# Gated graph network with attention on one core: sigmoid written through tanh, its affine part moved into VectorE's products

## The chip, the cores and the metric

The kernel runs on one core of one Trainium2 chip. The metric is device time in microseconds for one execution. A core has engines with queues of their own: TensorE (PE; its weight loads are PEld), VectorE (DVE), ScalarE (ACT), GpSimd (POOL) and SyncE (SP, which issues the DMAs). Each works through its queue in order and waits at semaphores for the others.

## The reference, cut to what matters

There are 128 graphs of 128 nodes with 256 features, in fp32, and an adjacency of zeros and ones for each graph. Layer 0 is a gated graph network of three rounds with shared gate weights, layer 1 an attention.

```python
h = jnp.maximum(_layernorm(x, axis=-1), 0.0)
for i in range(3):
    m = jnp.einsum('bnd,de->bne', h, weight[i])
    aggr = jnp.einsum('bst,bsd->btd', A, m)
    gi = aggr @ w_ih.T + b_ih;  gh = h @ w_hh.T + b_hh      # 3 * 256 columns each
    r = jax.nn.sigmoid(i_r + h_r)
    z = jax.nn.sigmoid(i_z + h_z)
    n = jnp.tanh(i_n + r * h_n)
    h = (1.0 - z) * n + z * h
x = x + h
h = jnp.maximum(_layernorm(x, axis=-1), 0.0)
Wh = h @ W;  s = Wh.sum(axis=-1)
e = jax.nn.leaky_relu(s[:, :, None] + s[:, None, :], negative_slope=0.2)
alpha = jax.nn.softmax(jnp.where(adj == 0, -jnp.inf, e), axis=-1)
return x + alpha @ Wh
```

## The kernel before

The 128 graphs are worked in 32 groups of four (`G = 4`). A group goes through three rounds, `layer` 0 to 2, so there are 96 phases (group, round). The list `turns` interleaves them: in the middle one phase each of group g, round 0; of g-1, round 1; and of g-2, round 2. A phase's gate products are planned at `SLOT` = 18150 ns of PE.

In rounds 0 and 1 the state is held transposed, in `hT` (features on the partitions, two halves j of 128, and 512 columns of four graphs times 128 nodes); in round 2 (`gru_rows`) the products come out with nodes on the partitions. `edge_sums` gives `aT`, the neighbours' sums, with matmuls in bf16 on three parts of each fp32 value. `node_sums` makes four sums and differences of blocks of `hT` and `aT` on POOL and DVE (`hs`, `gs`). From these `products` builds the gates by a scheme of seven block products in place of eight, in fp32 on PE. Its PSUM banks are X, Y and Q, each with one bank for r and z (`x_rz`, `y_rz`, `q_rz`) and one for the two parts of n (`x_n`, `y_n`, `q_n`: half 0 is h_n, half 1 is i_n). ACT copies X into Y (L702), and twice copies what Y holds to SBUF, as `t2` and `t3` (L692, `put`), while PE goes on adding to the same Y bank; DVE adds Q to these (L695). The four blocks that result lie in `T3`, `X`, `Y` and `T2`.

Then the gates, for each of the four blocks (j, n) in `gru`: ACT makes r with a sigmoid into `rz` (L740), DVE makes u = (h_n + bias) r (L743) and adds i_n (L747), and ACT makes z with another sigmoid (L750). For each half j ACT takes tanh of `u` (L756), and DVE makes d = h - n, d = d z and h = n + d (L759, L762, L764). `gru_rows` does the same with one sigmoid for r and z (L778), L782 and L786 for u, L795 for tanh and L797, L802 and L804 at the end; its biases are in PSUM already, since ACT seeds the banks with them (L687). `attention` follows the third round; its softmax takes the exps on ACT (L910).

The order of all engines is not that of the code: each `op(engine, ns, ...)` only notes an operation with a cost, and `Plan.run` orders them by a simulation, with PE's gate products at due times (`due`), the rest by how soon it is needed, and banks handed out in turn. The `exps` operation has a place of its own, right behind the copy of x_rz to y_rz of group g+2, round 1 (`turn=`), and its cost holds 2570 ns beside the exps for all groups but the last. `two=True` marks operations of DVE and POOL that the plan keeps from running at once.

Of the kernel before, what the change touches and what calls it, by code (L numbers as in the profile page):

```python
# [12 lines left out]
AF = mybir.ActivationFunctionType  # L13
OP = mybir.AluOpType
AX = mybir.AxisListType

P = 128
# [193 lines left out]
def kernel(  # L211
# [60 lines left out]
        "s_hh": (1, "all", const, [P, 7, 3, P]), "s_x0": (1, "all", const, [P, 7, 3, P]),  # L272
        "s_x1": (1, "all", const, [P, 7, 3, P]), "s_x2": (1, "all", const, [P, 7, 3, P]),
        "bias_i": (1, "all", const, [P, 3 * KD]), "bias_h": (1, "all", const, [P, 3 * KD]),
        "bias_s": (1, "all", const, [P, 3 * KD]),
        "seed_x": (1, "all", const, [P, 4, P]), "seed_q": (1, "all", const, [P, 4, P]),
        "w1": (1, "all", const, [P, KD, D]), "w1_out": (1, "all", const, [P, KD]),
        "w1_sum": (1, "all", const, [P, D]),
# [12 lines left out]
    def ap(b):  # L291
        return phys[(b.tag,) + b.slot]
# [13 lines left out]
    for kind in ("y_rz", "y_n"):  # L306
        y = phys[kind, 0, 0].rearrange("p q n -> p (q n)")
        for c in range(GN // P):
# [1 line left out]
                             skip_group_check=True)  # L310


    W = {t: buf(t) for t in ("s_hh", "s_x0", "s_x1", "s_x2", "bias_i", "bias_h", "bias_s", "seed_x",
                             "seed_q", "w1", "w1_out", "w1_sum")}
    spare = ["misc", "x_rz", "misc", "x_n", "misc", "q_rz", "misc", "q_n"]

# [56 lines left out]
    def weights():  # L373
# [18 lines left out]
        load_msg(1)  # L392
        for t, src in (("bias_i", b_ih), ("bias_h", b_hh)):
            load(W[t], ap, src.rearrange("(c p) -> p c", p=P), 500)
        op("DVE", 170, lambda: nc.vector.tensor_add(ap(W["bias_s"]), ap(W["bias_i"]),
                                                    ap(W["bias_h"])),
           [W["bias_i"], W["bias_h"]], [W["bias_s"]])

        w_hhT, w_ihT = [buf("u"), buf("u")], [buf("x1"), buf("x1")]
        turned(w_ih_nat, w_ihT, ("DVE", "ACT"))  # L400
# [271 lines left out]
    def products(layer, hT, hs, aT, gs, rows=False):  # L672

        five, seven, three, four = (7, 5, 4, 3) if rows else (5, 7, 3, 4)
        state, edges = (W["s_hh"], hT, hs), (W[f"s_x{layer}"], aT, gs)  # L680
        kinds = (("rz", ((R, (state, edges)), (Z, (state, edges)))),
                 ("n", ((NN, (state,)), (NN, (edges,)))))
        X, Y, Q, T2, T3 = ({} for _ in range(5))

        def seed(b, kind, t):
            q = 0 if kind == "rz" else 2
            op("ACT", 590, lambda: nc.scalar.copy(  # L687
                ap(b), ap(t)[:, q:q + 2].rearrange("p (o q) m -> p o (q m)", o=1)
                .to_broadcast([P, 2, 2 * P])), [t], [b])

        def put(t, y):
            op("ACT", 590, lambda: nc.scalar.copy(ap(t), ap(y)), [y], [t])  # L692

        def add(t, q):
            op("DVE", 690, lambda: nc.vector.tensor_tensor(ap(t), ap(t), ap(q), OP.add), [q], [t])  # L695

        for kind, parts in kinds:
            X[kind], Y[kind] = buf("x_" + kind), buf("y_" + kind)
            if rows:
                seed(X[kind], kind, W["seed_x"])  # L700
            product(X[kind], 1, parts, not rows, rows=rows)
            op("ACT", 590, lambda x=X[kind], y=Y[kind]: nc.scalar.copy(ap(y), ap(x)),  # L702
               [X[kind]], [Y[kind]], mark=(plan.group, layer, kind))
        for kind, parts in kinds:
            Q[kind] = buf("q_" + kind)
            if rows:
                seed(Q[kind], kind, W["seed_q"])
            product(Q[kind], five, parts, not rows, rows=rows)
        for kind, parts in kinds:
            product(Y[kind], 6, parts, False, rows=rows)  # L710
            T2[kind] = buf("t2_" + kind)
            put(T2[kind], Y[kind])
        for kind, parts in kinds:
            product(Y[kind], seven, parts, False, rows=rows)
            T3[kind] = buf("t3_" + kind)
            put(T3[kind], Y[kind])
# [10 lines left out]
        return (1, 1, T3), (0, 0, X), y + (Y,), t2 + (T2,)  # L727

    def gru(layer, hT, hs, aT, gs):

        blocks = products(layer, hT, hs, aT, gs)
        rz, u = buf("rz"), buf("u")

        def view(b, q=None):
            t = ap(b) if q is None else ap(b)[:, q]
            return t.rearrange("p (j n m) -> p j n m", j=KD, n=2)
        for j, n, src in blocks:
            cr, cz, cn, i = j, KD + j, 2 * KD + j, 2 * j + n
            s_rz, nn = src["rz"], src["n"]
            op("ACT", 511, lambda j=j, n=n, s_rz=s_rz, c=cr: nc.scalar.activation(  # L740
                view(rz, 0)[:, j, n, :], ap(s_rz)[:, 0, :], AF.Sigmoid, bias=ap(W["bias_s"])[:, c:c + 1]),
               [s_rz, W["bias_s"]], [(rz, i, i + 1)])
            op("DVE", 480, lambda j=j, n=n, nn=nn, c=cn: nc.vector.scalar_tensor_tensor(  # L743
                view(u)[:, j, n, :], ap(nn)[:, 0, :], ap(W["bias_h"])[:, c:c + 1], view(rz, 0)[:, j, n, :],
                op0=OP.add, op1=OP.mult), [nn, (rz, i, i + 1), W["bias_h"]], [(u, i, i + 1)],
               two=nn.tag[0] == "t")
            op("DVE", 422, lambda j=j, n=n, nn=nn: nc.vector.tensor_tensor(  # L747
                view(u)[:, j, n, :], view(u)[:, j, n, :], ap(nn)[:, 1, :], OP.add),
               [nn], [(u, i, i + 1)], two=nn.tag[0] == "t")
            op("ACT", 500, lambda j=j, n=n, s_rz=s_rz, c=cz: nc.scalar.activation(  # L750
                view(rz, 1)[:, j, n, :], ap(s_rz)[:, 1, :], AF.Sigmoid, bias=ap(W["bias_s"])[:, c:c + 1]),
               [s_rz, W["bias_s"]], [(rz, 4 + i, 5 + i)])
        for j in (1, 0):
            d, lo, hi = buf("d"), 2 * j, 2 * j + 2
            cols = slice(j * GN, (j + 1) * GN)
            op("ACT", 723, lambda j=j, cols=cols: nc.scalar.activation(  # L756
                ap(u)[:, cols], ap(u)[:, cols], AF.Tanh,
                bias=ap(W["bias_i"])[:, 2 * KD + j:2 * KD + j + 1]), [W["bias_i"]], [(u, lo, hi)])
# [3 lines left out]
            op("DVE", 690, lambda d=d, cols=cols: nc.vector.tensor_tensor(  # L762
                ap(d), ap(d), ap(rz)[:, 1, cols], OP.mult), [(rz, 4 + lo, 4 + hi)], [d], two=True)
            op("DVE", 690, lambda j=j, d=d, cols=cols: nc.vector.tensor_tensor(  # L764
                ap(hT)[:, j, :], ap(u)[:, cols], ap(d), OP.add), [(u, lo, hi), d], [(hT, lo, hi)], two=True)

    def gru_rows(layer, hT, hs, aT, gs, rows, x1):

        blocks = products(layer, hT, hs, aT, gs, rows=True)
        rz, u = buf("rz"), buf("u")  # L770

        def view(b):
# [1 line left out]
        for j, n, src in blocks:  # L774
# [2 lines left out]
            s_rz, nn = src["rz"], src["n"]  # L777
            op("ACT", 700, lambda outs=outs, graphs=graphs, s_rz=s_rz: nc.scalar.activation(  # L778
                ap(rz).rearrange("p q (g d) -> p g q d", g=G)[:, graphs, :, outs],
                ap(s_rz).rearrange("p g (q m) -> p g q m", q=2), AF.Sigmoid),  # L780
               [s_rz], [(rz, i, i + 1), (rz, 4 + i, 5 + i)])
            op("DVE", 422, lambda outs=outs, graphs=graphs, nn=nn: nc.vector.tensor_tensor(  # L782
                view(u)[:, graphs, outs], ap(nn)[:, :, 0:P],
                ap(rz)[:, 0].rearrange("p (g d) -> p g d", g=G)[:, graphs, outs], OP.mult),
               [nn, (rz, i, i + 1)], [(u, i, i + 1)], two=nn.tag[0] == "t")
            op("DVE", 422, lambda outs=outs, graphs=graphs, nn=nn: nc.vector.tensor_tensor(  # L786
                view(u)[:, graphs, outs], view(u)[:, graphs, outs], ap(nn)[:, :, P:2 * P], OP.add),
               [nn], [(u, i, i + 1)], two=nn.tag[0] == "t")
        for n in (1, 0):
            d, lo, hi = buf("d"), 2 * n, 2 * n + 2  # L790
# [2 lines left out]
            def part(b, lo=lo, hi=hi):  # L793
# [8 lines left out]
            op("DVE", 690, lambda d=d, cols=cols: nc.vector.tensor_tensor(  # L802
                ap(d), ap(d), ap(rz)[:, 1, cols], OP.mult), [(rz, 4 + lo, 4 + hi)], [d], two=True)
            op("DVE", 690, lambda d=d, part=part: nc.vector.tensor_tensor(  # L804
                part(x1), part(x1), ap(d), OP.add), [d], [(x1, lo, hi)], two=True)


    turns = [(0, 0), (1, 0), (2, 0), (0, 1), (1, 1), (3, 0), (0, 2), (2, 1), (1, 2)]
# [51 lines left out]
    def attention(g, a, x1, h1, lo, hi):  # L860
# [47 lines left out]
        def exps():  # L908
            for b in range(lo, hi):
                nc.scalar.activation(ap(e)[:, b, :], ap(e)[:, b, :], AF.Exp, bias=ap(low)[:, b:b + 1])  # L910
        op("ACT", 2570 * (g < NG - 1) + 320 * n, exps, [low], [e], turn=(g + 2, 1, "rz"))
        op("DVE", cost, lambda: nc.vector.tensor_reduce(small(den), es(), AX.X, OP.add), [e], [den])
        op("DVE", 170, lambda: nc.vector.reciprocal(small(rden), small(den)), [den], [rden])
        eT, uT = buf("eT"), buf("uT")
# [80 lines left out]
```

## Time and profile before

| | us |
|---|---|
| median of 3 runs | 2139.39 |
| lowest and highest | 2138.39, 2139.82 |
| the profiled execution | 2138.75 |
| its span, first to last instruction | 2136.9 |
| granted clock of TensorE, mean | 0.995 |

| engine | busy us | share |
|---|---|---|
| PE | 2108.1 | 99% |
| PEld | 1879.9 | 88% |
| DVE | 1750.7 | 82% |
| ACT | 1587.1 | 74% |
| POOL | 951.0 | 45% |

The shares are means over the whole span. Matmuls are pipelined, and their ends are modelled in the profile, so that the spacing of their starts says more than the busy time. Among the groups of ACT is ACT_TABLE_LOAD, an instruction that no line of the kernel writes: it is put before an activation whose function is not in the table set that the engine holds at that moment. A group's time is told with its count and the mean duration of one instruction; a "wait" is idle time of an engine before an instruction, put down to what ended it.

### The profile page before, as it was taken

Reading aid. Unit: us, or ns where it says so; the run is one execution under the profiler, and the core shown is the slowest. Engines: PE = TensorE matmul, PEld = TensorE weight load, DVE = VectorE, ACT = ScalarE, POOL = GpSimd, SP = SyncE. Lnnn points to the kernel's source line nnn. Section 1 sums busy time; section 2 is a strip of 40 time slices with the busy share of each in tenths; the row PEclk is TensorE's granted clock in tenths of the full one; section 3 lists DMA queues with packets and bytes.
Section 4 is the critical chain, followed back from the end, with each engine's and each line's share of the span. In section 5 each row is a group of like instructions: output and inputs, shape, how many; then the busy total and the mean of one; then the engine's idle time right before and its main releaser. Section 6 shows DMA issues by size and latency. Waiting matters only on the chain.

```text
span 2136.9 us, 33989 instructions
## 1 busy us (share of the span) xinstructions
PE 2108.1 (99%) x12550; PEld 1879.9 (88%) x12550; DVE 1750.7 (82%) x3297; ACT 1587.1 (74%) x2705; POOL 951.0 (45%) x889
## 2 busy tenths in 40 slices
PE   8999999999999999999999999999999999999997
PEld 7889888898888988889988889888888988988886
DVE  5677878788888889888898788888889888778777
ACT  5567877777877877777877777777777888676774
POOL 5545453445544445544344544355444454335421
PEclk9999999999999999999999999999999999999998
DMA  4222223232242312332222231313223323222221
GB/s 143 45 50 50 45 50 89 45 77 48 45 89 60 75 37 49 79 70 65 55 62 56 68 75 40 94 32 69 65 51 84 46 38 82 50 46 37 59 68 35
DMA packets 333430, 129.35 MB, mean 61 GB/s; under 512 B 264656, under 2 KB 333008, under 8 KB 333264
## 3 DMA queue, kind: packets, MB, share of 16 engines
q1 hardware_dynamic: 333264, 127.18, 27.1%
q8 instruction: 99, 1.62, 0.3%
q14 instruction: 67, 0.55, 0.1%
HBM read 45.36 MB, written 16.78 MB: 29 GB/s over the span
## 4 chain that ended last, share of the span: by engine, by line
PE 94%; DVE 3%; ACT 1%; DMA 1%; issue 1%; SPq 0%; DVEq 0%; ACTq 0%
PE y_rz L655 15%; PE q_rz L655 10%; PE x_rz L655 10%; PE y_rz L662 8%; PE y_n L655 7%; PE misc L597 6%; PE q_rz L662 5%; PE x_n L655 5%; PE x_rz L662 5%; PE q_n L655 5%; PE misc L935 5%; PE y_n L662 4%; PE misc L611 3%; PE x_n L662 3%; PE q_n L662 3%; PE misc L892 1%
## 5 line engine op out<-in xcount | busy, mean ns | idle before, releaser
L692 ACT COPY t_rz<-y_rz 128x512 f32<-128x512 f32 x192 | 112.3, 585 | 200.5 <-PE y_rz L662 104.9
L557 POOL TENSOR_TENSOR r<-rows 128x512 f32<-128x512 f32 x128 | 148.2, 1177 | 221.1 <-ACT rows L540 121.6
L625 POOL TENSOR_TENSOR hs<-hT 128x512 f32<-128x512 f32 x96 | 131.3, 1368 | 183.7 <-PE y_n L662 126.7
L655 PE MATMUL y_rz<-hs,s_hh 128*128 128x256 f32 x768 | 198.0, 380 | 2.6 <-ACT t_rz L692 2.6
L655 PE MATMUL y_rz<-gs,s_x 128*128 128x256 f32 x768 | 197.1, 379 | 0.0
L695 DVE TENSOR_TENSOR t_rz<-t_rz,q_rz 128x512 f32<-128x512 f32 x192 | 131.3, 684 | 69.4 <-PE q_rz L662 26.0
L582 POOL TENSOR_TENSOR pl<-d,pl 128x512 bf16<-128x512 f32 x64 | 77.9, 1219 | 217.8 <-ACT pl L580 217.7
L560 POOL TENSOR_TENSOR p<-r 128x512 bf16<-128x512 f32 x128 | 168.1, 1332 | 0.0
L655 PEld LDWEIGHTS y_rz<-gs,s_x 128*128 128x128 f32 x768 | 146.0, 190 | 19.8
L655 PEld LDWEIGHTS y_rz<-hs,s_hh 128*128 128x128 f32 x768 | 141.5, 190 | 21.8 <-ACT t_rz L692 4.0
L799 POOL TENSOR_TENSOR x<-x,u 128x512 f32<-128x512 f32 x64 | 88.1, 1379 | 143.0 <-ACT u L795 140.1
L695 DVE TENSOR_TENSOR t_n<-t_n,q_n 128x512 f32<-128x512 f32 x192 | 131.3, 684 | 22.5 <-ACT t_n L692 8.5
L629 POOL TENSOR_TENSOR hs<-hT,hs 128x256 f32<-128x256 f32 x96 | 74.1, 773 | 149.4 <-PE q_n L662 130.7
L577 POOL TENSOR_TENSOR d<-hT,pl 128x512 f32<-128x512 f32 x64 | 77.9, 1221 | 131.6 <-ACT pl L575 125.9
L692 ACT COPY t_n<-y_n 128x512 f32<-128x512 f32 x192 | 112.1, 584 | 29.5 <-PE y_n L655 16.8
L655 PE MATMUL x_rz<-hT,s_hh 128*128 128x256 f32 x512 | 131.5, 379 | 0.0
L655 PE MATMUL x_rz<-aT,s_x 128*128 128x256 f32 x512 | 131.5, 379 | 0.0
L935 PE MATMUL misc<-w,uT 128*128 128x256 f32 x512 | 121.7, 383 | 3.1 <-DVE e L898 1.7
L600 ACT COPY aT<-misc 128x512 f32<-128x512 f32 x192 | 110.6, 584 | 19.1 <-PE misc L597 13.7
L625 DVE TENSOR_TENSOR gs<-aT 128x512 f32<-128x512 f32 x96 | 96.8, 1009 | 27.4 <-ACT aT L600 27.4
L759 DVE TENSOR_TENSOR d<-hT,u 128x512 f32<-128x512 f32 x128 | 106.0, 828 | 12.2 <-ACT u L756 12.1
L655 PE MATMUL y_n<-hs,s_hh 128*128 128x256 f32 x384 | 114.5, 380 | 0.0
(215 smaller groups left out, 6548.9 us busy)
## 6 DMA issues: line engine op xcount, KB each, us to landing
rows<-in_x_dram SPq DMA_DIRECT2D x32, 512.0 KB, 4.2
x<-in_x_dram SPq DMA_DIRECT2D x32, 512.0 KB, 4.1
out_dram<-x SPq DMA_DIRECT2D x31, 512.0 KB, 3.0
at<-in_adj_dram SPq DMA_DIRECT2D x32, 256.0 KB, 2.8
plT<-pl SPq DMA_TRANSPOSE x186, 3.6
rz<-in_L_gnn_w_ih_dram SPq DMA_DIRECT2D x1, 768.0 KB, 5.0
rz<-in_L_gnn_w_hh_dram SPq DMA_DIRECT2D x1, 768.0 KB, 7.7
e<-in_L_gnn_weight_dram SPq DMA_DIRECT2D x3, 256.0 KB, 8.0
```

Source lines behind the costliest of these rows:

```text
L557: op("POOL", 1106, lambda part=part: nc.gpsimd.tensor_tensor(ap(r1)[:, part], ap(rows)[:, part], top(rows)[:, part], OP.subtract), [(rows, ...
L560: op("POOL", 1050, lambda part=part: nc.gpsimd.tensor_tensor(ap(p3)[:, part], ap(r1)[:, part], top(r1)[:, part], OP.subtract), [(r1, n, n ...
L597: nc.tensor.matmul(flat(ps)[:, b * N:(b + 1) * N], part(i, b, k), ap(a)[:, b, :], start=(i == 0), stop=(i == 2))
L600: op("ACT", 590, lambda k=k, ps=ps: nc.scalar.copy(ap(dst)[:, k, :], flat(ps)), [ps], [(dst, 2 * k, 2 * k + 2)])
L625: op(eng, cost, lambda: sub(ap(w)[:, 0:2, :], blocks()[:, 1::2, :], blocks()[:, 0:2, :], OP.subtract), [t], [(w, 0, 2)], two=True)
L655: nc.tensor.matmul(ap(bank)[:, half, :], ap(w)[:, i - 1, q, :], source(t, sums), start=(first and c == 0 and m == 0), stop=False, skip_gro ...
L662: nc.tensor.matmul(ap(bank)[:, m, half * P:(half + len(chunk)) * P], source(t, sums)[:, m * N:(m + 1) * N], ap(w)[:, i - 1, q:q + len(chun ...
L692: op("ACT", 590, lambda: nc.scalar.copy(ap(t), ap(y)), [y], [t])
L695: op("DVE", 690, lambda: nc.vector.tensor_tensor(ap(t), ap(t), ap(q), OP.add), [q], [t])
L759: op("DVE", 690, lambda j=j, d=d, cols=cols: nc.vector.tensor_tensor(ap(d), ap(hT)[:, j, :], ap(u)[:, cols], OP.subtract), [(hT, lo, hi), ...
L799: op("POOL", 1290, lambda cols=cols, part=part: nc.gpsimd.tensor_tensor(part(x1), part(x1), ap(u)[:, cols], OP.add), [(u, lo, hi)], [(x1, ...
L935: nc.tensor.matmul(ap(ps)[:, b, :], ap(uT)[:, k, (m + b) * N:(m + b + 1) * N], ap(w1)[:, k, :], start=(k == 0), stop=(k == KD - 1))
```

## The change

Sigmoid is written as sigmoid(v) = (tanh(v/2) + 1)/2, everywhere. ACT computes t = tanh(0.5 v + b/2), with the halved bias prepared once. The "+1" and the "/2" go into DVE's products: u becomes ((t + 1) h_n) 0.5 + i_n, and h becomes ((t_z + 1) d) 0.5 + n, as `scalar_tensor_tensor` instructions with two constants in place of `tensor_tensor` or of one with a bias column. The place of h_n's bias in that instruction is thus taken, so ACT adds the bias when it copies: `put` of x_n to y_n and of y_n to `t2_n` becomes two activations, one of half 0 with a bias column and one plain of half 1 (rounds 0 and 1 only). The X block, which is read from its bank and is not copied, gets a separate `tensor_scalar` for the "+1" and keeps the bias column. A small tensor `bias_n` holds the three bias columns. The 2570 ns are taken out of the planned cost of `exps`.

```diff
+        def half_bias():
+            nc.vector.tensor_add(ap(W["bias_s"]), ap(W["bias_i"]), ap(W["bias_h"]))
+            nc.vector.tensor_scalar(ap(W["bias_s"]), ap(W["bias_s"]), 0.5, None, op0=OP.mult)
+        op("DVE", 250, half_bias, [W["bias_i"], W["bias_h"]], [W["bias_s"]])
...
-        def put(t, y):
-            op("ACT", 590, lambda: nc.scalar.copy(ap(t), ap(y)), [y], [t])
+        def put(t, y, bias=None, mark=None):
+            if bias is None or rows:
+                op("ACT", 590, lambda: nc.scalar.copy(ap(t), ap(y)), [y], [t], mark=mark)
+                return
+            def halves():
+                nc.scalar.activation(ap(t)[:, 0], ap(y)[:, 0], AF.Identity,
+                                     bias=ap(W["bias_n"])[:, bias:bias + 1])
+                nc.scalar.copy(ap(t)[:, 1], ap(y)[:, 1])
+            op("ACT", 760, halves, [y, W["bias_n"]], [t], mark=mark)
...
-            op("ACT", 590, lambda x=X[kind], y=Y[kind]: nc.scalar.copy(ap(y), ap(x)),
-               [X[kind]], [Y[kind]], mark=(plan.group, layer, kind))
+            put(Y[kind], X[kind], 1 if kind == "n" else None, mark=(plan.group, layer, kind))
...
-            put(T2[kind], Y[kind])
+            put(T2[kind], Y[kind], 2 if kind == "n" else None)
...
-                view(rz, 0)[:, j, n, :], ap(s_rz)[:, 0, :], AF.Sigmoid, bias=ap(W["bias_s"])[:, c:c + 1]),
-               [s_rz, W["bias_s"]], [(rz, i, i + 1)])
+                view(rz, 0)[:, j, n, :], ap(s_rz)[:, 0, :], AF.Tanh, bias=ap(W["bias_s"])[:, c:c + 1],
+                scale=0.5), [s_rz, W["bias_s"]], [(rz, i, i + 1)])
+            if src is X:
+                op("DVE", 290, lambda j=j, n=n: nc.vector.tensor_scalar(
+                    view(rz, 0)[:, j, n, :], view(rz, 0)[:, j, n, :], 1.0, None, op0=OP.add),
+                   [], [(rz, i, i + 1)])
+                op("DVE", 480, lambda j=j, n=n, nn=nn: nc.vector.scalar_tensor_tensor(
+                    view(u)[:, j, n, :], ap(nn)[:, 0, :], ap(W["bias_n"])[:, 0:1], view(rz, 0)[:, j, n, :],
+                    op0=OP.add, op1=OP.mult), [nn, (rz, i, i + 1), W["bias_n"]], [(u, i, i + 1)])
+            else:
+                op("DVE", 480, lambda j=j, n=n, nn=nn: nc.vector.scalar_tensor_tensor(
+                    view(u)[:, j, n, :], view(rz, 0)[:, j, n, :], 1.0, ap(nn)[:, 0, :],
+                    op0=OP.add, op1=OP.mult), [nn, (rz, i, i + 1)], [(u, i, i + 1)],
+                   two=nn.tag[0] == "t")
-            op("DVE", 422, lambda j=j, n=n, nn=nn: nc.vector.tensor_tensor(
-                view(u)[:, j, n, :], view(u)[:, j, n, :], ap(nn)[:, 1, :], OP.add),
+            op("DVE", 422, lambda j=j, n=n, nn=nn: nc.vector.scalar_tensor_tensor(
+                view(u)[:, j, n, :], view(u)[:, j, n, :], 0.5, ap(nn)[:, 1, :], op0=OP.mult, op1=OP.add),
...
-                ap(d), ap(d), ap(rz)[:, 1, cols], OP.mult), [(rz, 4 + lo, 4 + hi)], [d], two=True)
+            op("DVE", 690, lambda d=d, cols=cols: nc.vector.scalar_tensor_tensor(
+                ap(d), ap(rz)[:, 1, cols], 1.0, ap(d), op0=OP.add, op1=OP.mult),
...
-                ap(hT)[:, j, :], ap(u)[:, cols], ap(d), OP.add), [(u, lo, hi), d], [(hT, lo, hi)], two=True)
+            op("DVE", 690, lambda j=j, d=d, cols=cols: nc.vector.scalar_tensor_tensor(
+                ap(hT)[:, j, :], ap(d), 0.5, ap(u)[:, cols], op0=OP.mult, op1=OP.add),
...
-        op("ACT", 2570 * (g < NG - 1) + 320 * n, exps, [low], [e], turn=(g + 2, 1, "rz"))
+        op("ACT", 320 * n, exps, [low], [e], turn=(g + 2, 1, "rz"))
```

The two gate products of `gru_rows` and its last two (L782, L786, L802, L804) change in the same manner, and its sigmoid (L778) becomes a tanh with scale 0.5.

More of the change, by code (lines that the diff above doesn't have):

```diff
@@ L274 @@
         "bias_i": (1, "all", const, [P, 3 * KD]), "bias_h": (1, "all", const, [P, 3 * KD]),
-        "bias_s": (1, "all", const, [P, 3 * KD]),
+        "bias_s": (1, "all", const, [P, 3 * KD]), "bias_n": (1, "all", const, [P, 3]),
         "seed_x": (1, "all", const, [P, 4, P]), "seed_q": (1, "all", const, [P, 4, P]),
@@ L310 @@
                              skip_group_check=True)
-    W = {t: buf(t) for t in ("s_hh", "s_x0", "s_x1", "s_x2", "bias_i", "bias_h", "bias_s", "seed_x",
+    W = {t: buf(t) for t in ("s_hh", "s_x0", "s_x1", "s_x2", "bias_i", "bias_h", "bias_s", "bias_n", "seed_x",
                              "seed_q", "w1", "w1_out", "w1_sum")}
@@ L394, in weights, with n_bias @@
             load(W[t], ap, src.rearrange("(c p) -> p c", p=P), 500)
-        op("DVE", 170, lambda: nc.vector.tensor_add(ap(W["bias_s"]), ap(W["bias_i"]),
-                                                    ap(W["bias_h"])),
-           [W["bias_i"], W["bias_h"]], [W["bias_s"]])
+        def half_bias():
+            nc.vector.tensor_add(ap(W["bias_s"]), ap(W["bias_i"]), ap(W["bias_h"]))
+            nc.vector.tensor_scalar(ap(W["bias_s"]), ap(W["bias_s"]), 0.5, None, op0=OP.mult)
+        op("DVE", 250, half_bias, [W["bias_i"], W["bias_h"]], [W["bias_s"]])
+        def n_bias():
+            nc.vector.tensor_copy(ap(W["bias_n"])[:, 0:2], ap(W["bias_h"])[:, 2 * KD:3 * KD])
+            nc.vector.tensor_tensor(ap(W["bias_n"])[:, 2:3], ap(W["bias_h"])[:, 2 * KD:2 * KD + 1],
+                                    ap(W["bias_h"])[:, 2 * KD + 1:2 * KD + 2], OP.subtract)
+        op("DVE", 250, n_bias, [W["bias_h"]], [W["bias_n"]])
         w_hhT, w_ihT = [buf("u"), buf("u")], [buf("x1"), buf("x1")]
@@ L726, in products @@
         y, t2 = ((0, 1), (1, 0)) if rows else ((1, 0), (0, 1))
-        return (1, 1, T3), (0, 0, X), y + (Y,), t2 + (T2,)
+        return ((1, 1, T3), (0, 0, X), y + (Y,), t2 + (T2,)), X
     def gru(layer, hT, hs, aT, gs):
-        blocks = products(layer, hT, hs, aT, gs)
+        blocks, X = products(layer, hT, hs, aT, gs)
         rz, u = buf("rz"), buf("u")
@@ L740, in gru @@
             op("ACT", 511, lambda j=j, n=n, s_rz=s_rz, c=cr: nc.scalar.activation(
-                view(rz, 0)[:, j, n, :], ap(s_rz)[:, 0, :], AF.Sigmoid, bias=ap(W["bias_s"])[:, c:c + 1]),
-               [s_rz, W["bias_s"]], [(rz, i, i + 1)])
[L743 to L746, printed above, removed]
@@ L749, in gru @@
+            op("DVE", 422, lambda j=j, n=n, nn=nn: nc.vector.scalar_tensor_tensor(
+                view(u)[:, j, n, :], view(u)[:, j, n, :], 0.5, ap(nn)[:, 1, :], op0=OP.mult, op1=OP.add),
                [nn], [(u, i, i + 1)], two=nn.tag[0] == "t")
             op("ACT", 500, lambda j=j, n=n, s_rz=s_rz, c=cz: nc.scalar.activation(
-                view(rz, 1)[:, j, n, :], ap(s_rz)[:, 1, :], AF.Sigmoid, bias=ap(W["bias_s"])[:, c:c + 1]),
-               [s_rz, W["bias_s"]], [(rz, 4 + i, 5 + i)])
+                view(rz, 1)[:, j, n, :], ap(s_rz)[:, 1, :], AF.Tanh, bias=ap(W["bias_s"])[:, c:c + 1],
+                scale=0.5), [s_rz, W["bias_s"]], [(rz, 4 + i, 5 + i)])
@@ L761, in gru @@
                [(hT, lo, hi), (u, lo, hi)], [d], two=True)
-            op("DVE", 690, lambda d=d, cols=cols: nc.vector.tensor_tensor(
-                ap(d), ap(d), ap(rz)[:, 1, cols], OP.mult), [(rz, 4 + lo, 4 + hi)], [d], two=True)
-            op("DVE", 690, lambda j=j, d=d, cols=cols: nc.vector.tensor_tensor(
-                ap(hT)[:, j, :], ap(u)[:, cols], ap(d), OP.add), [(u, lo, hi), d], [(hT, lo, hi)], two=True)
+            op("DVE", 690, lambda d=d, cols=cols: nc.vector.scalar_tensor_tensor(
+                ap(d), ap(rz)[:, 1, cols], 1.0, ap(d), op0=OP.add, op1=OP.mult),
+               [(rz, 4 + lo, 4 + hi)], [d], two=True)
+            op("DVE", 690, lambda j=j, d=d, cols=cols: nc.vector.scalar_tensor_tensor(
+                ap(hT)[:, j, :], ap(d), 0.5, ap(u)[:, cols], op0=OP.mult, op1=OP.add),
+               [(u, lo, hi), d], [(hT, lo, hi)], two=True)
     def gru_rows(layer, hT, hs, aT, gs, rows, x1):
-        blocks = products(layer, hT, hs, aT, gs, rows=True)
+        blocks, _ = products(layer, hT, hs, aT, gs, rows=True)
         rz, u = buf("rz"), buf("u")
@@ L779, in gru_rows @@
                 ap(rz).rearrange("p q (g d) -> p g q d", g=G)[:, graphs, :, outs],
-                ap(s_rz).rearrange("p g (q m) -> p g q m", q=2), AF.Sigmoid),
+                ap(s_rz).rearrange("p g (q m) -> p g q m", q=2), AF.Tanh, scale=0.5),
                [s_rz], [(rz, i, i + 1), (rz, 4 + i, 5 + i)])
-            op("DVE", 422, lambda outs=outs, graphs=graphs, nn=nn: nc.vector.tensor_tensor(
-                view(u)[:, graphs, outs], ap(nn)[:, :, 0:P],
-                ap(rz)[:, 0].rearrange("p (g d) -> p g d", g=G)[:, graphs, outs], OP.mult),
+            op("DVE", 422, lambda outs=outs, graphs=graphs, nn=nn: nc.vector.scalar_tensor_tensor(
+                view(u)[:, graphs, outs],
+                ap(rz)[:, 0].rearrange("p (g d) -> p g d", g=G)[:, graphs, outs], 1.0,
+                ap(nn)[:, :, 0:P], op0=OP.add, op1=OP.mult),
                [nn, (rz, i, i + 1)], [(u, i, i + 1)], two=nn.tag[0] == "t")
-            op("DVE", 422, lambda outs=outs, graphs=graphs, nn=nn: nc.vector.tensor_tensor(
-                view(u)[:, graphs, outs], view(u)[:, graphs, outs], ap(nn)[:, :, P:2 * P], OP.add),
+            op("DVE", 422, lambda outs=outs, graphs=graphs, nn=nn: nc.vector.scalar_tensor_tensor(
+                view(u)[:, graphs, outs], view(u)[:, graphs, outs], 0.5, ap(nn)[:, :, P:2 * P],
+                op0=OP.mult, op1=OP.add),
                [nn], [(u, i, i + 1)], two=nn.tag[0] == "t")
@@ L801, in gru_rows @@
                [(u, lo, hi)], [(x1, lo, hi)])
[L802 to L805, printed above, removed]
+            op("DVE", 690, lambda d=d, cols=cols: nc.vector.scalar_tensor_tensor(
+                ap(d), ap(rz)[:, 1, cols], 1.0, ap(d), op0=OP.add, op1=OP.mult),
+               [(rz, 4 + lo, 4 + hi)], [d], two=True)
+            op("DVE", 690, lambda d=d, part=part: nc.vector.scalar_tensor_tensor(
+                part(x1), ap(d), 0.5, part(x1), op0=OP.mult, op1=OP.add), [d], [(x1, lo, hi)], two=True)
     turns = [(0, 0), (1, 0), (2, 0), (0, 1), (1, 1), (3, 0), (0, 2), (2, 1), (1, 2)]
```

## The prediction

> **What bounds the kernel now.** I read the page's first two parts, then the table by stretches, the waits of PE, the groups with their shapes kept apart, and last the timeline where PE stood still.
>
> ```profile
> PE 2108.1 (99%) x12550; PEld 1879.9 (88%) x12550; DVE 1750.7 (82%) x3297; ACT 1587.1 (74%) x2705; POOL 951.0 (45%) x889
> ...
> 1000.00:1200.00 200.00, 200.00 (x1199) 179.44 (x1198) 170.96 (x319) 154.35 (x259) 90.33 (x84) 1.00 0.26 62
> ...
> 2100.00:2137.00 37.00, 22.65 (x96) 17.22 (x94) 24.73 (x64) 11.04 (x24) 4.10 (x6) 0.82 0.13 43
> ```
>
> The columns of the stretches are length, then busy PE, PEld, DVE, ACT, POOL. In the middle PE is busy for all of 200 us while ACT has 46 us to spare and DVE 29; the two stretches that are not full are the first 50 us (42.60 busy) and the last 37 (22.65 busy). A busy PE need not be a fast one, so I looked at the spacing of its starts in the timeline: four matmuls of 256 columns start 0.86 to 0.87 us after the four before, the whole way, at a granted clock of 1.00. PE runs at its own rate, and the change takes no instruction from it. What can be won is what PE waits for. Of the waits from 100 us to 2070 us these are the ones over 0.2 us:
>
> ```profile
> PE y_rz L655 <- ACT t_rz L692: 2.6, 3, 1.4
> PE y_rz L662 <- ACT t_rz L692: 1.4, 1, 1.4
> PE x_rz L662 <- ACT x_rz L687: 1.2, 1, 1.2
> PE misc L935 <- DVE x L940: 1.0, 1, 1.0
> PE misc L597 <- ACT uT L616: 0.8, 1, 0.8
> ```
>
> Columns: total us, times, longest. That is 7.0 us in all, 6.0 of them for ACT. Two have a table load on ACT just ahead:
>
> ```profile
> 224.63 1.28 ACT L778 ACT_TABLE_LOAD   x1
> 225.92 0.63 ACT L778 ACTIVATE rz<-t_rz 128x512 f32<-128x512 f32 x1
> 226.46 0.61 ACT L795 ACTIVATE u<-u 128x512 f32<-128x512 f32 x1
> 226.98 0.56 ACT L692 COPY t_rz<-y_rz 128x512 f32<-128x512 f32 x1
> 227.59 1.13 PE L655 MATMUL y_rz<-hs,s_hh 128*128 128x256 f32 x4 [1.35 <-ACT t_rz L692]
> ...
> 1896.16 1.28 ACT L750 ACT_TABLE_LOAD   x1
> 1898.98 0.70 PE L662 MATMUL x_rz<-s_hh,hT 128*128 128x256 f32 x2 [1.24 <-ACT x_rz L687]
> ```
>
> The copy that PE waits for stands behind the load in ACT's order. The waits of 0.97 us at 249.44 and 0.24 us at 1890.56 are another thing: there ACT itself had waited for DVE (L747) at the head of its queue.
>
> **The change, part by part.**
>
> *Table loads.* The groups have 63 loads of 1283 ns: 31 at L910 (before the exps), 31 before a sigmoid (L778 29, L740 1, L750 1), and the first. Does tanh need none next to exp? The timeline of ACT shows it:
>
> ```profile
> 462.82 1.28 ACT L910 ACT_TABLE_LOAD   x1
> 464.12 1.28 ACT L910 ACTIVATE e<-e,low 128x128 f32<-128x128 f32 x4
> ...
> 467.47 0.73 ACT L756 ACTIVATE u<-u,bias_i 128x512 f32<-128x512 f32 x1
> ...
> 469.15 1.28 ACT L778 ACT_TABLE_LOAD   x1
> 470.45 0.63 ACT L778 ACTIVATE rz<-t_rz 128x512 f32<-128x512 f32 x1
> ```
>
> Tanh (L756) runs behind exp with no load, the sigmoid (L778) needs one. So 62 go. A load occupies 462.80 to 464.12, 1.31 us with its edges: 62 x 1.31 = 81 us off ACT. The Trainium skill (ScalarE: Activation LUTs, What ACT_TABLE_LOAD costs) adds a drain of about 1380 ns to each switch, 2.66 us in all, which would make 165 us. The rows show no such gap on either side, so I take 81. On the path either figure is worth only the two waits above, 1.35 + 1.24 = 2.6 us, since all the other loads lie beside a full PE.
>
> *Tanh in place of sigmoid, 640 activations.* Equal: at 128x512 from SBUF without bias the sigmoid of L778 takes 632 ns and the tanh of L795 627. The constant scale of 0.5 has no row; bounds are 0 and the 0.10 us that a bias column adds (467 ns at L750 from x_rz against 366 for L616's copy of the same size), 64 us over all. I take 0.
>
> *h_n's bias in ACT's copies.* 64 copies of x_n to y_n (578 ns) and 64 of y_n to t_n (584) become two halves: one with a bias, 467 ns (L750), one plain, 366 (L616), less the overlap of neighbours, 0.10 us (four L496 of 594 ns take 2.06). That is 0.73, or +0.15 us x 128 = +19 us. Behind the y_n copy lie PE's q products and y_rz (4.3 us); behind the t_n copy eight y_rz matmuls of 1.73 us before PE returns to that bank, and the copy is over about 1.0 us after PE left it. Cover gone, it would cost 0.15 us each. ACT's balance: -81 + 19 = -62, to 1525 (71%); with the scale at its upper bound ACT stands where it is.
>
> *DVE.* Added: 64 tensor_scalar of 128x256 on the X block; nearest row L886, 294 ns at that size: +19 us, or +55 if POOL is met on the port (L828 of twice the size averages 865). Removed: the bias column at 192 scalar_tensor_tensor, 483 ns against 421 for L747's plain sum from PSUM: -12 us. The other products turn from tensor_tensor to scalar_tensor_tensor with constants. Here a rule speaks against the change: the Trainium skill (Vector Engine (DVE) Microarchitecture Reference, Points that are easy to get wrong) says that this form with two SBUF sources which are not bf16 runs at half throughput. Those are 256 + 128 instructions of 128x512 and 128 + 128 of 128x256; at one more pass (0.26 us per 256 columns, from 421 to 684 ns) that is 384 x 0.53 + 256 x 0.26 = 270 us, and DVE would stand at 2030. The rows say otherwise:
>
> ```profile
> L868 DVE SCALAR_TENSOR_TENSOR hw<-h,w_sum x128: 413/425/1376, 211.8 to 2120.9; 128x256 f32<-128x256 f32 x128
> L901 DVE SCALAR_TENSOR_TENSOR e<-e x33: 424/692/1530, 216.8 to 2123.9; 128x512 f32<-128x512 f32 x31, 128x256 f32<-128x256 f32 x2
> L764 DVE TENSOR_TENSOR hT<-u,d x128: 678/691/1807, 51.0 to 2037.3; 128x512 f32<-128x512 f32 x128
> ```
>
> Minimum/median/maximum ns: 425 and 692 with two fp32 sources from SBUF, as the plain sum of L764. I take no extra; DVE becomes 1758 us, at most about 1795. It lies beside PE. If the cover were gone, the X block's step lengthens by 0.3 us one chain r, u, tanh, d, hT; but x_n's bank is next written 5.2 us (24 matmuls) later and its readers need about 2. Two small bias instructions at the start (0.2 us each, L395's row) come 14 us before their first use. POOL's and SP's queues keep their instructions and DMAs; nothing is moved past them.
>
> *The order.* It is made by a planner from costs, and the change replaces 3850 by 1280 ns for the exps of all groups but the last, so everything near them may shift. In the middle there is nothing to gain from a better order, PE being full. In the tail there is: PE stands 5.1 us before L922 at 2110.08 for a bank that DVE frees late in its own order, behind u, d, x and st of another group:
>
> ```profile
> 2110.08 1.08 PE L922 MATMUL misc<-ident,e 128*128 128x128 f32 x4 [5.13 <-DVE x L940]
> ```
>
> The exps just before had been planned 2.6 us too dear: their load at 2102.38 hid in a wait for L905. I give half of the stall, 2.5 us, as an estimate; bounds are +4 (a worse shuffle, about the present wait again) and -5.1.
>
> *Sum.* -2.6 - 2.5 = -5.1 us. The profiled execution took 2138.75 (span 2136.9 and 1.85 around it), so 2133.65; the median is 0.64 higher, 2134.3. I say 2134.
>
> **The rivals.** *No change (0.27).* The two waits pass to the next late thing, for instance DVE's u (as at 249.44), and the tail comes out as long as before: 2139. For it: PE is at 99%, and 60 of 62 loads are hidden. Against: two stalls have the load itself as the last cause.
>
> *Slower by the y bank (0.13).* PE returns to y_rz 0.86 us after leaving it (four y_n matmuls); the t_rz copy takes 0.585, starts 0.20 after PE's next product (2089.37 against 2089.17), and PE follows its end by 0.05 (227.54, 227.59), so 0.03 us are spare, and whatever ACT does at that moment is paid in full. If the longer t_n and y_n copies are planned ahead of a t_rz copy, each costs 0.15 us and up: 64 phases make 10 us, 2149. It decides from 29 phases (4.3 us). Against: ACT sits idle 200.5 us before its 192 t_rz copies, 1.25 us at each of the 160 waits, and only four or so are late today.
>
> *A form at a bad price (0.02).* The halved throughput, or a bias copy (Identity, not in this trace) outside exp's table set, with two loads of 1.31 us at each of 128 copies, 335 us on ACT: DVE at 95%, or ACT at 87% in long pieces; some 2% lost, by estimate, 2180. The rows of L868 and L901 exclude the first nearly; the second has no row.
>
> **How the numbers follow.** About 0.2%, 4.3 us, is what a measurement of this kernel can tell from no change. The likeliest case (0.58) centres on 2134 and reaches past 2135.1 only in its weak part, which I count under no change. If all the waits of the middle (7.0) and the tail's 5.1 went, and a little of the last waits, it would be 2124; that is the low end. The high end takes in most of the bank case, to 2146. Outside I leave about 0.06 below and 0.1 above. Faster 0.58, same 0.27, slower 0.15.
>
> **What would show it.** Right: one ACT_TABLE_LOAD; ACT near 1525 us and DVE 1755 to 1795; PE still 2108 busy; no wait of PE at the old places of 227 and 1899; L922's wait in the tail shorter; scalar_tensor_tensor of 128x512 at a median near 690 ns. Wrong: a second kind of load; those at 950 or more; many short waits of PE y_rz or y_n on ACT's L692; or a time under 2124, which could only come from PE itself, whose starts would then stand closer than 0.216 us.

## The result, and the profile after

| | before | after |
|---|---|---|
| median, us | 2139.61 (2138.39 to 2140.66) | 2129.27 (2128.28 to 2131.72) |
| ratio, with 95% interval | | 0.9954 (0.9936 to 0.9971) |
| profiled execution, us | 2138.75 | 2131.72 |
| its span, us | 2136.9 | 2129.0 |

The change saves 10.3 us by the medians, 0.46% by the ratio. In a second measurement the changed kernel came to 2129.83 against 2139.00, that is 9.2 us less and the same ratio of 0.9954 (0.9942 to 0.9967). The experiments were measured in three series on three chips, each with runs of the kernel before beside it (medians 2139.92, 2139.00 and 2139.05), so what a kernel saves is told against the kernel before of its own series. The profiled execution of the changed kernel is the slowest of its four.

First the busy times on the page of the changed kernel:

```profile
PE 2108.4 (99%) x12550; PEld 1882.8 (88%) x12550; DVE 1701.3 (80%) x3364; ACT 1536.5 (72%) x2771; POOL 923.8 (43%) x889
```

PE is busy for the same 2108 us with the same 12550 matmuls; what was saved is idle PE. ACT lost 51 us, and DVE, which the forecast had gaining 7 us, lost 49. The groups of ACT hold one table load, the one at the start:

```profile
L351 ACT ACT_TABLE_LOAD x1 | 1.3, 1283 | 0.7 <-PEq L1012 0.7
```

Line numbers have moved: 663 and 670 are the gate products (655 and 662 before), 702 the plain copies, 941 the exps. PE's waits in the middle (100 to 2070 us) are these (total us, times, longest):

```profile
PE q_rz L670 <- ACT q_rz L695: 1.2, 1, 1.2
PE misc L605 <- ACT aT L608: 0.7, 1, 0.7
```

Of the five waits of the middle shown before, 7.0 us, none is left at its place; the two that stand here, 1.9 us together, are new ones (at about 198 and 2045 us).

The longest waits of the tail (from 2070 us):

```profile
PE misc L953 <- DVE x L971: 2.7, 1, 2.7
PE misc L953 <- ACT e L941: 1.8, 1, 1.8
```

The 5.1 us in front of the transposes (L922 before, L953 now) have become 2.7, but L953 now also waits 1.8 us for the exps of the last group. All waits of the tail come to 8.0 us where there were 10.0, yet the tail as a whole is not shorter. These lines are the first and the last work of PE behind its last gate product, before and then after (where the first is the line of 2090.78, shown in the last section):

```profile
2099.71 1.89 PE L935 MATMUL misc<-w,uT 128*128 128x256 f32 x8
2130.54 2.24 PE L935 MATMUL misc<-w,uT 128*128 128x256 f32 x8
...
2122.68 2.24 PE L966 MATMUL misc<-w,uT 128*128 128x256 f32 x8
```

That is 33.1 us before and 34.1 after (33.1 in a second profile of the changed kernel). PE reaches its tail 8.9 us earlier, and that is where the gain lies.

In the table by stretches, one from 400 to 1800 us, PE busy is the second number:

```profile
400.00:1800.00 1400.00, 1400.00 (x8395) 1256.75 (x8394) 1138.60 (x2256) 1045.49 (x1865) 615.84 (x590) 1.00 0.28 63
```

### The profile page after: what moved, and what is told of

Its sections match the earlier page's. It is cut to its first block, busy times and chain, and to the rows that moved or that the text cites. A ratio compares the mean times of both kernels' runs of the same rounds, so it can differ in the third digit from the quotient of the medians.

```text
span 2129.0 us, 34073 instructions
## 1 busy us (share of the span) xinstructions
PE 2108.4 (99%) x12550; PEld 1882.8 (88%) x12550; DVE 1701.3 (80%) x3364; ACT 1536.5 (72%) x2771; POOL 923.8 (43%) x889
## 5 line engine op out<-in xcount | busy, mean ns | idle before, releaser
L565 POOL TENSOR_TENSOR r<-rows 128x512 f32<-128x512 f32 x128 | 140.4, 1117 | 229.8 <-ACT rows L548 99.9
L568 POOL TENSOR_TENSOR p<-r 128x512 bf16<-128x512 f32 x128 | 159.6, 1267 | 0.0
L829 POOL TENSOR_TENSOR x<-x,u 128x512 f32<-128x512 f32 x64 | 82.5, 1305 | 100.1 <-DMA x<-in_x_dram 54.9
L785 DVE TENSOR_TENSOR d<-hT,u 128x512 f32<-128x512 f32 x128 | 115.4, 901 | 10.5 <-ACT u L782 10.5
L663 PE MATMUL y_n<-gs,s_x 128*128 128x256 f32 x384 | 114.3, 379 | 0.0
L966 PEld LDWEIGHTS misc<-w,uT 128*128 128x128 f32 x512 | 98.6, 196 | 15.6 <-ACT uT L624 2.1
```

The lines of the kernel that those rows point to most:

```text
L565: op("POOL", 1106, lambda part=part: nc.gpsimd.tensor_tensor(ap(r1)[:, part], ap(rows)[:, part], top(rows)[:, part], OP.subtract), [(rows, ...
L568: op("POOL", 1050, lambda part=part: nc.gpsimd.tensor_tensor(ap(p3)[:, part], ap(r1)[:, part], top(r1)[:, part], OP.subtract), [(r1, n, n ...
L663: nc.tensor.matmul(ap(bank)[:, half, :], ap(w)[:, i - 1, q, :], source(t, sums), start=(first and c == 0 and m == 0), stop=False, skip_gro ...
L966: nc.tensor.matmul(ap(ps)[:, b, :], ap(uT)[:, k, (m + b) * N:(m + b + 1) * N], ap(w1)[:, k, :], start=(k == 0), stop=(k == KD - 1))
```

## Experiments: loads and order taken apart

The change does two things to time at once: it takes 62 loads off ACT, and through the planned costs (above all 2570 ns less for each of 31 exps) it gives all engines another order. Five kernels separate these. Two of them swap the activation function alone, so that every queue keeps the order of its parent.

**The function alone, in the kernel before.**

```diff
-                view(rz, 0)[:, j, n, :], ap(s_rz)[:, 0, :], AF.Sigmoid, bias=...
+                view(rz, 0)[:, j, n, :], ap(s_rz)[:, 0, :], AF.Tanh, bias=...
```

The same at the other two sigmoids.

> The kernel before with the tanh function in place of the sigmoid in its three activations and nothing else: every engine keeps its order, only the 62 table loads go (r and z are then a tanh, so another function is computed). Theory A (the loads stood in the way): the two stalls of PE behind a load, 1.35 and 1.24 us, go, and ACT is at 1587 - 81 = 1506 us: 2137 us, 2.6 below before. Theory B (the new order made the gain): the same 2.6 at most, because the other waits and the tail stay where they are; the other 7.7 us are the order's. Theory C (the loads upset everything behind them, so that DVE and POOL meet less often once they are gone): 2130 or less, with DVE below 1720 us.

Measured: 2135.66 us, ratio 0.9979 (0.9971 to 0.9987), that is 4.3 us less by the medians; the interval of the ratio makes 2.8 to 6.2. Theories A and B gave 2.6. ACT fell from 1587.1 to 1508.0, 79.1 us for 62 loads, 1.28 us each. DVE did not move:

```profile
PE 2109.5 (99%) x12550; PEld 1883.5 (88%) x12550; DVE 1752.2 (82%) x3297; ACT 1508.0 (71%) x2643; POOL 952.1 (45%) x889
```

The theory that loads upset DVE and POOL falls with that. PE's waits from 100 to 2070 us are down to these:

```profile
PE y_rz L662 <- ACT t_rz L692: 1.3, 1, 1.3
PE y_rz L655 <- ACT t_rz L692: 1.1, 2, 0.8
PE misc L935 <- DVE x L940: 1.0, 1, 1.0
PE misc L597 <- DMA plT<-pl: 0.7, 1, 0.7
```

That is 4.1 us where there were 7.2, with a wait of 0.2 us on a DMA that the prediction's list left out and that is 0.7 here. The two behind a load are gone. They cost PE more than the list says. PE runs the same matmuls in the same order in both kernels, so their starts (the first number of a row; the second is the duration) can be set side by side. Across the first stall, in the kernel before:

```profile
225.65 0.60 PE L655 MATMUL y_n<-gs,s_x 128*128 128x256 f32 x2
228.56 1.03 PE L655 MATMUL y_rz<-gs,s_x 128*128 128x256 f32 x4
```

and without loads:

```profile
225.06 0.59 PE L655 MATMUL y_n<-gs,s_x 128*128 128x256 f32 x2
226.49 1.03 PE L655 MATMUL y_rz<-gs,s_x 128*128 128x256 f32 x4
```

PE falls behind by 1.48 us where the list has 1.35, and by 1.51 across the stall at 1899 us, where it has 1.24. The list counts a wait from the modelled end of the matmul before, and that lies late: these matmuls start 0.22 us apart and are booked with 0.38 us each. A wait of 0.77 us at 2054 (L597 behind ACT's uT) went too. From 200 us to the tail this kernel gains 3.7 us on the one before. Between the stalls the two run level, so the other values that it computes cost PE nothing.

**The function alone, in the changed kernel.**

```diff
-                view(rz, 0)[:, j, n, :], ap(s_rz)[:, 0, :], AF.Tanh, bias=ap(W["bias_s"])[:, c:c + 1],
+                view(rz, 0)[:, j, n, :], ap(s_rz)[:, 0, :], AF.Sigmoid, bias=ap(W["bias_s"])[:, c:c + 1],
                 scale=0.5), ...
```

> The changed kernel with the sigmoid function in place of its three scaled tanh activations and nothing else: every engine keeps the new order, only the 62 loads come back (r and z are computed wrongly by this). Theory A: 2129.3 plus what loads cost, 2.6 us or more as the new plan has no room for them (exps priced 2.57 us lower): 2132 to 2140. Theory B: 2132 at most, most of the gain stays. Theory C: 2139 and DVE back at 1750 us.

Measured: 2138.60 us, 0.9992 (0.9984 to 1.0000): 1.3 us saved where the changed kernel saves 9.2 and 10.3, nearly the whole gain given back, by loads alone in an unchanged order. That speaks against the theory that the order by itself made the gain. DVE stays at 1704.4, so its fall is not the loads' doing either. What the loads do in this order is seen in PE's waits between 400 and 1800 us:

```profile
PE y_rz L663 <- ACT y_rz L702: 2.1, 9, 0.2
PE misc L605 <- DVE x L971: 0.5, 1, 0.5
```

and in the timeline of one of the nine:

```profile
732.23 1.28 ACT L941 ACT_TABLE_LOAD   x1
733.52 1.28 ACT L941 ACTIVATE e<-e,low 128x128 f32<-128x128 f32 x4
734.71 0.61 ACT L825 ACTIVATE u<-u 128x512 f32<-128x512 f32 x1
735.34 1.28 ACT L806 ACT_TABLE_LOAD   x1
736.63 0.63 ACT L806 ACTIVATE rz<-t_rz 128x512 f32<-128x512 f32 x1
737.17 1.03 ACT L985 COPY pe<-e 128x1024 uint16<-128x1024 uint16 x1
738.10 0.58 ACT L702 COPY y_rz<-x_rz 128x512 f32<-128x512 f32 x1
...
738.00 0.59 PE L663 MATMUL q_n<-gs,s_x 128*128 128x256 f32 x2
738.82 1.10 PE L663 MATMUL y_rz<-hs,s_hh 128*128 128x256 f32 x4 [0.23 <-ACT y_rz L702]
739.76 1.03 PE L663 MATMUL y_rz<-gs,s_x 128*128 128x256 f32 x4
```

From the first load to the copy of x_rz are 5.87 us, 2.6 of them loads. PE, done with x_rz and x_n, has only the q products to do before it needs that copy, and comes 0.23 us too early. In the changed kernel the same row of work, without loads, reads:

```profile
727.52 1.28 ACT L941 ACTIVATE e<-e,low 128x128 f32<-128x128 f32 x4
728.70 0.62 ACT L825 ACTIVATE u<-u 128x512 f32<-128x512 f32 x1
729.22 0.62 ACT L806 ACTIVATE rz<-t_rz 128x512 f32<-128x512 f32 x1
729.74 1.03 ACT L985 COPY pe<-e 128x1024 uint16<-128x1024 uint16 x1
730.68 0.58 ACT L702 COPY y_rz<-x_rz 128x512 f32<-128x512 f32 x1
...
733.40 0.59 PE L663 MATMUL q_n<-gs,s_x 128*128 128x256 f32 x2
734.70 1.03 PE L663 MATMUL y_rz<-gs,s_x 128*128 128x256 f32 x4
```

The copy begins 3.16 us after the exps began, and is ahead of PE by the q products (they start at 731.24 and last 2.6 us). From the q_n products to the second part of y_rz PE takes 1.30 us here and 1.76 with the loads, so that each such stall costs it 0.46 us, twice the 0.23 on the list. Over the middle these add up. Two matmul groups with the loads:

```profile
420.12 1.03 PE L663 MATMUL x_rz<-aT,s_x 128*128 128x256 f32 x4
1756.89 0.61 PE L670 MATMUL y_n<-s_x,gs 128*128 128x128 f32 x4
```

and the same two in the changed kernel:

```profile
416.90 1.03 PE L663 MATMUL x_rz<-aT,s_x 128*128 128x256 f32 x4
1747.99 0.61 PE L670 MATMUL y_n<-s_x,gs 128*128 128x128 f32 x4
```

PE is 3.2 us late at the first and 8.9 at the second. Of the 3.2 us 1.9 arose between 200 and 400 us; 1.4 are of the first 100 us, where two executions of the changed kernel also differ. By the tail it is 9.5 us late. From 200 us to the tail it thus loses 8.1 us, of the 7.9 to 9.0 that the loads cost in all; some 4 of these are the nine waits for the copy of x_rz.

**The price alone, in the kernel before.**

```diff
-        op("ACT", 2570 * (g < NG - 1) + 320 * n, exps, [low], [e], turn=(g + 2, 1, "rz"))
+        op("ACT", 320 * n, exps, [low], [e], turn=(g + 2, 1, "rz"))
```

> The kernel before with the planned cost of the exps lowered as in the change (2570 ns taken out) and nothing else: the sigmoid and its loads stay, the order of all engines is new. Theory A: no gain, 2139 or some us more, as the plan now has no room for loads that are still there. Theory B: a good part of the 10 us, 2132 to 2135. Theory C: as A, DVE near 1750 us.

Measured: 2141.15 us, 1.0006 (0.9998 to 1.0014): no gain. Its list of waits has the same 9 waits of PE for the copy of x_rz:

```profile
PE y_rz L655 <- ACT y_rz L702: 2.1, 9, 0.2
```

DVE, however, is at 1685.0, so the order alone lowers it.

**The price alone, in the changed kernel** (the same line the other way round).

> The changed kernel with the old planned cost of the exps (2570 ns put back) and nothing else: no loads but the first, another order. Theory A: 2129 to 2131, the loads are gone. Theory B: the truer cost made the gain, so 2135 to 2137. Theory C: 2129 to 2131 with DVE near 1700 us.

Measured: 2134.97 us, 0.9979 (0.9971 to 0.9988): 5.0 us saved, about half of what the changed kernel saves, with DVE at 1764.6. Theory A missed by 4 us; the time lies at the edge of what theory B gave. The waits in its middle, of which the second stands in the changed kernel too:

```profile
PE q_rz L670 <- DVE gs L633: 3.2, 1, 3.2
PE q_rz L670 <- ACT q_rz L695: 1.2, 1, 1.2
PE y_n L670 <- ACT t_n L702: 1.2, 1, 1.2
```

**Loads and price together, without the new forms:** the kernel before with both edits, function and price.

> The kernel before with the tanh function in place of the sigmoid and the exps' planned cost lowered, and nothing else: the plan and order of the run with cheap exps, without its 62 loads; none of the new forms of DVE and ACT (r and z are a tanh, so another function is computed). Theory A (loads and their price in the plan are the whole gain): 2129 to 2132, as the changed kernel, with no short waits of PE y_rz on the copy of x_rz. Rival (the new forms take part, by another balance of ACT and DVE): 2134 or more.

Measured: 2131.30 us, 0.9962 (0.9949 to 0.9974). The interval holds the change's own 0.9954. One wait of PE over 0.2 us is left in the middle (1.3 us). What each kernel saves in us, median against the median of the kernel before in its own series, with DVE's busy time behind the stroke:

| | exps planned at 3850 ns | exps planned at 1280 ns |
|---|---|---|
| sigmoid, old forms | 0 / 1751 (before) | -1.2 / 1685 |
| sigmoid, new forms | not run | 1.3 / 1704 |
| tanh, old forms | 4.3 / 1752 | 7.7 / 1678 |
| tanh, new forms | 5.0 / 1765 | 9.2 and 10.3 / 1704 and 1701 (changed) |

Taking the loads away is worth 4.3 us in the old plan and 7.9 to 9.0 in the new; lowering the price is worth 3.4 us (old forms) and 4.2 to 5.4 (new forms) without loads, and nothing with them (old forms). The price's worth lies in the middle: the listed waits of PE there are 4.1 us at the old price and 1.3 at the new with the old forms, 5.8 and 1.9 with the new forms. Each price is the right one for its kernel: with loads the block of exps takes 1.28 + 2 x 1.31 = 3.90 us, and 3850 was planned; without them it takes 1.28.

## Experiments: the new forms by themselves

**scalar_tensor_tensor with neutral constants**, at the seven places of the change, in the order of before:

```diff
-                ap(d), ap(d), ap(rz)[:, 1, cols], OP.mult), ...
+                ap(d), ap(rz)[:, 1, cols], 0.0, ap(d), op0=OP.add, op1=OP.mult), ...
```

> The kernel before with the new form alone: scalar_tensor_tensor with neutral constants (1 for a product, 0 for a sum) at the seven places where the change puts it for tensor_tensor, same order on all engines. Theory A (the form costs the same): 2140 as before, DVE within 5 us of 1751, 128x512 at a median near 690 ns. Rival (half the rate with two fp32 sources in SBUF): DVE near 2020 us, and the time 2180 or more.

Measured: 2139.03 us, 1.0000 (0.9992 to 1.0008), DVE 1751.5. The group of L762, minimum, median and maximum ns:

```profile
L762 DVE SCALAR_TENSOR_TENSOR d<-rz,d x128: 659/692/1747, 52.3 to 2038.6; 128x512 f32<-128x512 f32 x128
```

Before, as tensor_tensor, it stood at 657/692/1750. Half throughput does not happen here.

**The copies in two halves**, with the bias column gone from DVE's product in three blocks, planned costs and order as before:

```diff
-            op("ACT", 590, lambda: nc.scalar.copy(ap(t), ap(y)), [y], [t])
+            def halves():
+                nc.scalar.activation(ap(t)[:, 0], ap(y)[:, 0], AF.Identity,
+                                     bias=ap(W["bias_n"])[:, bias:bias + 1])
+                nc.scalar.copy(ap(t)[:, 1], ap(y)[:, 1])
+            op("ACT", 590, halves, [y], [t], mark=mark)
```

> The kernel before with the biased copies alone: the 128 copies of h_n and i_n in two halves, one with the bias, and the bias column gone from DVE's product in three blocks of four; planned costs and order as before, sigmoid and loads stay. Theory A (hidden): 2140 within 1, ACT 1587 + 19 = 1606 us. Rival (each longer copy is paid at the y bank): up to 128 x 0.15 = 19 us, 2144 to 2159, with new waits of PE y_rz or y_n on L692's place.

Measured: 2139.75 us, 1.0004 (0.9995 to 1.0012); ACT 1609.2, or 22 us more, DVE 1744.8, or 6 less. PE's waits from 100 us on are those of before within 0.2 us each. The longer copies cost nothing.

The second measurement of the changed kernel, whose numbers stand in the first section:

> The changed kernel once more, beside the others on one chip, for a closer interval. All theories: 2129 to 2130, ratio 0.995 to 0.9955.

## Experiments: is there more to have

**Two more prices set right**, in the changed kernel:

```diff
-                op("DVE", 480, lambda j=j, n=n, nn=nn: nc.vector.scalar_tensor_tensor(
+                op("DVE", 422, lambda j=j, n=n, nn=nn: nc.vector.scalar_tensor_tensor(
...
-                   [], [(rz, i, i + 1)])
+                   [], [(rz, i, i + 1)], two=True)
```

> The changed kernel with two planned prices set to what its profile shows: DVE's product without a bias column at 422 instead of 480 ns, and the tensor_scalar of the X block marked[...] (634 ns on average where 290 was planned). If the plan's truth about small items is worth something: 2127 to 2129, and DVE's tensor_scalar nearer to 300 ns. If the exps were the only price that mattered: 2129 to 2131, another draw of start and tail.

Measured: 2130.59 us, 0.9958 (0.9944 to 0.9972), which cannot be told from the changed kernel. The tensor_scalar of the X block averaged 592 ns, not near 300, so the mark did little for it. A price off by 60 ns decides nothing here; that of the exps was off by 2570.

**The exps' fixed place taken away**, in the changed kernel:

```diff
-        op("ACT", 320 * n, exps, [low], [e], turn=(g + 2, 1, "rz"))
+        op("ACT", 320 * n, exps, [low], [e])
```

> The changed kernel with the exps' fixed place (right behind the copy of x_rz to y_rz) taken away, so that the plan places them by need. That place was for a block of ACT work with two loads; without loads it may cost more than it gives. If the place still matters (1.28 us on ACT at a bad moment delays a copy that PE waits for): 2131 or more, with waits of PE on ACT copies. If not: 2127 to 2130.

Measured: 2207.85 us, 1.0324 (1.0310 to 1.0338). The expectation of harm was right in sign and far too small, and it named the wrong place. PE's longest waits:

```profile
PE misc L619 <- ACT eT L989: 35.4, 5, 8.7
PE x_n L663 <- DVE u L773: 11.0, 1, 11.0
```

PE does not wait for a delayed copy of x_rz but for the exps' own result. The timeline shows the path at one such place: exps at 623.56, the copy to planes (L985), a DMA transpose issued at 625.94, the copy back (L989) at 629.84, and only then the matmuls of L619 at 631.22, 7.7 us after the exps began. In the changed kernel the exps of 727.52 have their L619 at 757.73, 30 us later, and PE waits for none of it. The fixed place sets the exps early enough to hide that path, so it has another use than room for the loads.

No version of these beat the changed kernel.

## Why the prediction came out right, and which terms were mis-sized

The forecast was 2134 with a range of 2124 to 2146, and a faster kernel; measured were 2129.3. The gain came to about twice the 5.1 us of the forecast's sum: both of its terms were too small, and one stood at the wrong place, so it is the wide range that held. Point by point:

- *What bounds it.* Right. PE's busy time and count are the same, and all of the gain is idle PE.
- *62 loads gone, 81 us of ACT.* Right: 79.1 us by the run that swaps only the function. The drain that the Trainium skill adds (ScalarE: Activation LUTs, What ACT_TABLE_LOAD costs) does not show in ACT's busy time or in gaps around the loads: in the timeline above a load of 1.28 us stands from 732.23 and the exps begin at 733.52.
- *The loads' worth on the path.* Mis-sized: 2.6 us were given for two stalls; the run at the old order shows 4.3, interval 2.8 to 6.2. The two stalls did go. In PE's starts they were worth 3.0 us, not 2.6, because the list of waits undercounts them, and a third wait on ACT of 0.8 us went with them. Little of this passed to the next late thing: one wait on a DMA grew from 0.2 to 0.7 us.
- *The order.* The cause was named, the price of 2570 ns; its worth was mis-sized and its place was wrong. The forecast gave 2.5 us in the tail and nothing in the middle, PE being full there. The runs with and without the price show 3.4 to 5.4 us, in the middle: at the old price PE waits 3.2 us at one q_rz and 1.2 at a y_n, for instance. The tail's stall shrank from 5.1 to 2.7 us as forecast, but a new wait and slower matmuls behind it took that back, and the tail as a whole gained nothing. That the term had the right sign for the time is luck, since its reason did not hold. And the two terms are not a sum of independent parts: the lower price is worth something only without loads, and the loads cost about twice as much under it, 0.46 us at a time.
- *Same time for tanh and the constant scale at 0.* Right: 629 ns for L806 with scale where the sigmoid took 632.
- *Biased copies, +19 us on ACT, hidden.* Right: +22 and no time. The rival of the y bank finds no support; t_rz waits did not multiply. ACT as a whole ended at 1536.5, not 1525; most of the difference is the new order, which adds 8 us in the two runs with tanh and old forms (1508.0 and 1516.4).
- *DVE at 1758.* Wrong: 1701. The parts were as told: 418 and 421 ns for the forms without a bias column from PSUM, 6 us saved in the run with halved copies. The tensor_scalar of the X block lay between its bounds, 634 ns on average. What outweighs both is how often DVE meets POOL. In the traces, instruction by instruction, that tensor_scalar takes 287 ns on average where no POOL instruction runs beside it and 905 where one does; L743's product of t_n in the kernel before takes 477 and 989. Of its 128 instances 84 meet one before and 66 with the price alone changed, where form and function are those of before, and the average falls from 813 ns to 602. Every run planned at 3850 has DVE between 1745 and 1765, every one at 1280 between 1678 and 1713. So it comes from the order. For the time it has no weight: the run with DVE at 1685 and the loads in place took 2141.
- *Half throughput of the new form.* Excluded by its own run: 692 ns at the median with either form.

Left over are 1.5 us between the run with loads and price alone (2131.30) and the changed kernel of the same series (2129.83), five executions each; the intervals do not separate them. Whether the new forms have a small part in the gain stays open.

## What to carry to other kernels

When an engine with slack sits beside a full one, do not count its busy time but ask where the full engine waits for it; 79 us off ACT were worth 4 to 9 us here. Read the cost of a stall from PE's starts in two kernels of the same order, not from the wait alone. Where an order is planned from costs, a change of an operation and its price belong together: the price of what is gone takes half the gain, and the new price over the old operation gives none. To take such a pair apart, edit the function without touching costs, then costs without the function.

## What the runs showed of the hardware

In the tail PE's granted clock fell after a stall. In the changed kernel the same group of 16 matmuls took 3.62 us at 2090.78 and then, after PE had stood for 2.65 us and more, 6.72:

```profile
2090.78 3.62 PE L966 MATMUL misc<-w,uT 128*128 128x256 f32 x16
...
2104.32 6.72 PE L966 MATMUL misc<-w,uT 128*128 128x256 f32 x16 [0.68 <-ACT uT L624]
```

The granted clock, the number before the last two, was 1.00 ahead of the stall and 0.50 behind it:

```profile
2090.00:2094.00 4.00, 4.00 (x24) 3.64 (x23) 3.89 (x8) 0.81 (x2) 0.89 (x1) 1.00 0.00 0
2097.00:2104.00 7.00, 5.24 (x20) 4.28 (x20) 6.63 (x19) 1.93 (x5) 2.21 (x4) 0.50 0.05 16
2092.00:2129.00 37.00, 24.86 (x88) 18.86 (x86) 21.14 (x59) 9.26 (x22) 3.79 (x5) 0.70 0.12 43
```

The forecast had not priced this. Over the last 37 us the clock was 0.82 before and 0.70 after (0.75 in the second profile of the changed kernel), and what the shorter stall saved was paid back in slower matmuls. In the kernel with the freed exps the stretches of 200 us in which PE stood for about 10 us, such as 1000 to 1200, have a clock of 0.97 where the changed kernel has 1.00. PE's busy time for the same matmuls is 2125.8 us there against 2108.4, so long waits came with slower matmuls beside their own length.
